# Three edits to a planned decoder kernel: mask order, cross-attention maxima from block-diagonal keys, a free choice of evicting engine

## The chip, the cores and the metric

One core of a Trainium2 chip. The time is device microseconds of one execution, the median of the runs shown. Before the change: 1095.75 us, from three runs of 1095.5, 1095.75 and 1112.12 us.

## What is computed

A decoder layer on x of 2 x 1024 tokens, 256 features, all in float32, in three residual steps:

```python
x = x + attn(layernorm(x))              # causal self-attention, then a "liquid" recurrence, then a GELU MLP
x = x + xattn(layernorm(x), ctx, ctx)   # cross-attention over 77 context tokens
x = x + ffn(layernorm(x))               # 8 binary trees of depth 7, each node a hidden unit
```

- `attn` works on two sequences of 1024 tokens with 16 heads of 16 features. Its scores are causal; the output is projected, the liquid step iterates `tanh(ctx @ w_ctx + xs @ w_x + b)` eight times, and an MLP of 1024 hidden units follows.
- `xattn` has 16 heads of 16 features as well, with 77 keys and values for each of the two sequences and no mask: `softmax(q k / 4) v`, then a projection.
- `ffn` has eight trees of 255 nodes; only the nodes on each token's path count.

A softmax here subtracts the row's maximum before the exponential. The largest edit concerns how cross-attention finds these maxima.

## The kernel before, in words

**Blocks and threads.** The 2048 tokens are cut into four blocks of 512 (`TB`). Each block has four chains of work, written as Python generators: `scores` (layernorm, query/key/value projections, the maxima of the causal scores), `values` (scores again with keys in the partitions, exponential, product with the values), `middle` (liquid recurrence, MLP, cross-attention, layernorm) and `leaves` (the trees). `prepare` runs once, ahead of block 0's `middle`, and makes a product of two weights (`w_ac`), a bias (`b_ac`), and the cross-attention's keys `xk` and values `xv`.

**The planner.** The order of instructions on PE (TensorE), ACT, DVE and POOL is fixed when the program is built. `Clock` keeps an account of when each engine, tile and PSUM bank would be free, by costs written into the class. `weave` (L283) looks at all chains, asks `choices` (L234) for what each could do next, and takes the step with the earliest start plus a "worth", ties going to the chain that is furthest behind its due place. DMAs all go through SP's queue in the order in which the program issues them.

**Heads in slots.** A head has 16 features, but each head's queries and keys stand in a slot of 32 partitions (`SLOT`), four heads to 128 partitions (`NG` = 4 groups). Odd rows hold features, row 0 holds the row maximum (in q) against a constant 1 (in k), so that the scores come out with the maximum subtracted. A product of one head is a matmul on 32 rows of PE's array. Four heads sit in four different row strips and run at the same time when they are issued one after the other. `Heads` (L68) describes such a unit; `choices` may issue two heads of one unit, four of one, or a mixed set: two heads of a unit that ACT will read (exponentials) and two of a unit that DVE will read (maxima). `issue` (L262) writes the matmuls. For a causal diagonal tile it first writes the mask into the bank as a bf16 matmul `mask x ident` over the whole array, step 0, and then accumulates the scores, step 1:

```python
for step in range(max(len(unit.steps) for unit, _, _ in heads)):
    for unit, j, ps in reversed(heads):
        if step < len(unit.steps):
            unit.one(j, ps, unit.steps[step])
```

**Cross-attention's maxima** (`cross_attention`, L897). Queries go through `project_slots` (L578): a projection into a tile, and four DMAs (L197) that spread it into the slots of `xq`. Then, for each of 4 pieces of 128 tokens (`qi`), one `Heads` unit makes 16 scores of 128 queries by 77 keys, one head at a time on 32 rows, four groups into the same bank of each head (L907). DVE reduces each bank, 4 x 77 columns to 4 maxima, four times; PE transposes the 512 maxima (L923), and `shift` (L652) puts them into row 0 of the queries: `q * head + pt`, where `head` is 0 in row 0 and 1 elsewhere. The exponentials' scores are made afterwards with the keys in the partitions (L948). There are 4 blocks x 4 pieces = 16 such rounds.

**Evictions.** A PSUM bank that only has to be copied out (with or without a scale and a bias) goes to a fixed engine: column half 0 to ACT, half 1 to DVE in `features_first` (L524) and `project_slots`; always to ACT in `weigh` (L609); one half each in `trees` (L999).

**Startup.** Weights are loaded in a fixed order (L394 to L412): `vecs`, block 0's x, `woT`, `w_ctx`, `wq`, `wk`, `wv`, `vrow` (five bias rows, 640 KB as broadcast), `ctxT`, `xwk`, `xwv` and the rest. `prepare` computes `w_ac`, then `b_ac`, then keys and values.

Of the kernel before, what the change touches and what calls it, by code (L numbers as in the profile page):

```python
# [40 lines left out]
for _name, _k in (  # L41
    ("g_attn", 2), ("b_attn", 2), ("bq", 2), ("bk", 2), ("out_b", 2), ("g1", 2), ("b1", 2),
    ("b_inl", 2), ("g2", 2), ("b2", 2), ("ff_b1", 8), ("xbq", 2), ("xbk", 4),
    ("b_in", 2 * PAR), ("rights", 2), ("shift", 1), ("head", 1),
):
    _COLS[_name] = (_n, _k)
    _n += _k
# [8 lines left out]
}  # L56

# [10 lines left out]
class Heads:  # L68
# [3 lines left out]
    def __init__(self, banks, one, read, engine, steps=(0,)):  # L72
        self.banks, self.one, self.read, self.engine, self.steps = banks, one, read, engine, steps
        self.left = [0, 2] if engine == "dve" else [2, 0]
        self.reads = []


class Clock:
# [10 lines left out]
    def __init__(self, nc):  # L89
        self.nc = nc  # L90
        self.pe = 0.0
        self.dma = 1.0
        self.at = {"act": 0.0, "dve": 0.0, "pool": 0.0, "dma": 0.0}
        self.written = {}
        self.used = {}
        self.banks = [0.0] * 8
        self.table = None
        self.mode = (P, P)
        self.share = 4
        self.children = []  # L100
# [49 lines left out]

    def transpose(self, out, x, ident):
        self.array(0.109, (P, P), out, x)
        return self.nc.tensor.transpose(out, x, ident)  # L153

    def array(self, cost, mode, out, *ins):
        cost += self.REARRANGE if (SLOT in mode or SLOT in self.mode) and mode != self.mode else 0.0
        self.mode = mode
        self.pe = max(self.pe, self.ready(ins) + self.HANDOVER) + cost
        self.note(self.pe + 0.14, out, ins)

# [38 lines left out]
    def load(self, out, src):  # L199
        self.dma = max(self.dma, self.pe - 6) + max(out.free_size() * 4 * P / 300e3, 0.5)  # L200
        self.note(self.dma + 2.0, out, ())
        self.nc.sync.dma_start(out=out, in_=src)
# [18 lines left out]
    def start(self, need):  # L221


        if isinstance(need, Op):
            return self.when(need)
        aps, kind = need
        if callable(kind):
            return self.pe if kind() else float("inf")
        at = max(self.pe, self.ready(aps) + self.HANDOVER)
        if kind:  # L230
            at = max(at, self.free_banks()[kind - 1][0])
        return at

    def choices(self, t, todo):  # L234

        need = t["need"]
        if isinstance(need, Op) or not isinstance(need[1], Heads):
            at = self.start(need)
            if isinstance(need, Op) or not need[0]:
                return [(at, 0.0, None)]  # L240
            return [(at, max(0.0, self.ready(need[0]) + self.MARGIN - at), None)]
# [7 lines left out]
        found.append((max(self.pe, ready, free[1][0]) + self.ALONE, 0.0, [(own, own.left[0])]))  # L249
        if len(own.left) == 2:  # L250
            found.append((two, 0.0, [(own, 0), (own, 2)]))
        for u in todo:
            other = None if isinstance(u["need"], Op) else u["need"][1]
            if not isinstance(other, Heads) or other.engine == own.engine:
                continue
            at = max(two, self.ready(u["need"][0]) + self.HANDOVER)
            for j0 in own.left:
                if 2 - j0 in other.left:
                    found.append((at, -self.MIXED, [(own, j0), (other, 2 - j0)]))
        return found  # L260

    def issue(self, heads):  # L262
# [5 lines left out]
        for step in range(max(len(unit.steps) for unit, _, _ in heads)):  # L268

            for unit, j, ps in reversed(heads):  # L270
                if step < len(unit.steps):
                    unit.one(j, ps, unit.steps[step])
# [10 lines left out]
    def weave(self, *threads):  # L283
# [25 lines left out]
        while todo:  # L309
# [9 lines left out]
            if heads:  # L319
                pe = self.pe = max(self.pe, at - self.ALONE if len(heads) == 1 else at)  # L320
                self.issue(heads)
                for t in todo:
                    if not isinstance(t["need"], Op):
                        share = sum(u is t["need"][1] for u, _ in heads) / len(heads)
                        t["done"][0] += share * (self.pe - pe)
            elif isinstance(need, Op):
                self.run(need)
# [14 lines left out]
def decoder_kernel(ctx: ExitStack, tc: tile.TileContext, ins: dict, out: bass.AP):  # L342
# [60 lines left out]
    vrow = const.tile([P, 5, D], F32, tag="vrow", name="vrow")  # L403
    clock.load(vrow.rearrange("p i d -> p (i d)"), ins["vrows"][0:1, :].to_broadcast([P, 5 * D]))
    ctxT = load("ctxT", (DC, B * T), **d)
    xwk = load("xwk", (DC, NG * P), **d)
    xwv = load("xwv", (DC, D), **d)
    wo = load("wo", (DC, D))
# [14 lines left out]
    mask32 = work.tile([P, P], F32, tag="mask32", name="mask32", bufs=1)  # L423
# [21 lines left out]
    xk = [const.tile([P, NG, T], F32, tag=f"xk{b}", name=f"xk{b}") for b in range(B)]  # L445
# [78 lines left out]
    def features_first(dst, src, name, g=None, b=None):  # L524

        for c in range(DC):
# [6 lines left out]
            if g is None:  # L533
                if c == 0:
                    yield clock.activation(dst[:, c, :], ps, AF.Copy)
                else:
                    yield clock.vector("tensor_copy", dst[:, c, :], ps)
            elif c == 0:
                yield clock.activation(dst[:, c, :], ps, AF.Identity, bias=col(b, c), scale=col(g, c))
            else:  # L540
                yield clock.vector("tensor_scalar", dst[:, c, :], ps, col(g, c), col(b, c), ALU.mult, ALU.add)
# [21 lines left out]
    def project_heads(dst, w, bias, src, n, name):  # L563

        for half in range(2):
            for i in range(2):
                g = 2 * half + i
                yield (src,), 2 if i == 0 else None
                if i == 0:
                    ps = banks(2)  # L570
                mm_cols(ps[i][:, :n], w, src, slice(g * P, (g + 1) * P), n)
                if i == 0:
                    yield clock.activation(dst(g), ps[i][:, :n], AF.Identity, bias=col(bias, g))
                else:
                    yield clock.vector("tensor_scalar", dst(g), ps[i][:, :n], col(bias, g), None, ALU.add)
            clock.free(*ps)

    def project_slots(dst, w, bias, src, tile, name):  # L578

        for c in range(DC):  # L580
# [3 lines left out]
            if c == 0:  # L584
                yield clock.activation(tile[:, c, :], ps, AF.Identity, bias=col(bias, c))
            else:
                yield clock.vector("tensor_scalar", tile[:, c, :], ps, col(bias, c), None, ALU.add)
# [7 lines left out]
    def project_values(dst, src, w, row, n, name):  # L595
# [3 lines left out]
        for c in range(DC):  # L599
# [4 lines left out]
            vrow[:n, row, :].rearrange("p (h d) -> p h d", d=HD),  # L604
# [4 lines left out]
    def weigh(at, av, g, name):  # L609
# [3 lines left out]
        yield clock.activation(raw, av, AF.Copy)  # L613
# [38 lines left out]
    def shift(q, pt):  # L652

        yield clock.vector("scalar_tensor_tensor", q, q, col("head", 0), pt, ALU.mult, ALU.add)


    def norms(tb, x, h0):
# [8 lines left out]
        yield from add_row(h0, 2)  # L666
        block[tb]["xn"] = xn

    def queries(tb):
# [9 lines left out]
        for i in range(NQ):  # L679
            cols = slice(i * P, (i + 1) * P)  # L680
            yield from project_values(v[:, blk * NQ + i], xn[:, :, cols], wv, 0, P, f"v{tb}_{i}")
# [58 lines left out]
    def weighted(tb, g, qT, at):  # L740
# [8 lines left out]
        def with_values():  # L749
            for kc in range(last + 1):  # L750
                yield (), lambda: step["made"] >= kc
                off = offset(kc)
                yield p[kc].values(), 1 if kc == 0 else None
# [109 lines left out]
    def feed_forward(tb, x, h0):  # L863
        hn = yield from layernorm(h0, f"l2_{tb}", "g2", "b2")
        yield clock.vector("tensor_tensor", x, x, h0, ALU.add)
        yield from add_row(x, 3)
# [30 lines left out]
    def cross_attention(tb, x):  # L897
        k, values = xk[tb // BPB], xv[tb // BPB]
        xn = yield from layernorm(x, f"x{tb}")
        yield from add_row(x, 4)  # L900
        yield from project_slots(xq, xwq, "xbq", xn, dtile(f"xqc{tb}"), f"xq{tb}")
        for qi in range(NQ):
            nm = nmax[2 + qi % 2]
            slots = nm.rearrange("p g (j s) -> p j g s", s=SLOT)
            cols = slice(qi * P, (qi + 1) * P)

            def scores(j, ps, g):  # L907
                r = slice(j * SLOT, (j + 1) * SLOT)
                clock.matmul(
                    ps[:, g * T : (g + 1) * T], xq[r, g, cols], k[r, g, :], start=True, stop=True  # L910
                )

            def read(j, ps):
                return [clock.vector(
                    "tensor_reduce", slots[:, j, :, 0],
                    ps[:, : NG * T].rearrange("p (g t) -> p g t", t=T), AX.X, ALU.max, negate=True,
                )]

            yield (xq[:, :, cols],), Heads(banks, scores, read, "dve", range(NG))
# [10 lines left out]
        def with_values():  # L930
            for g in range(NG):
                yield (), lambda: step["made"] >= g
                yield p[g].values(), 1
# [11 lines left out]
        for g in range(NG):  # L945
            p[g] = {}

            def one(j, ps, _):  # L948
                r = slice(j * SLOT, (j + 1) * SLOT)
                clock.matmul(ps[:T, :], k[r, g, :], xq[r, g, :], start=True, stop=True)  # L950
# [16 lines left out]
    def trees(tb):  # L967
# [5 lines left out]
        def outwards():  # L973


            for t in range(0, PAR, 2):
# [22 lines left out]
                if t == 0:  # L999
                    yield clock.activation(y[:, 0, :], po[0][:, :], AF.Copy)  # L1000
                    yield clock.vector("tensor_copy", y[:, 1, :], po[1][:, :])
# [48 lines left out]
    def prepare():  # L1050
        yield (woT, w_ctx), 2
        ps = banks(2)
        for dc in range(DC):
            for c in range(DC):
                clock.matmul(
                    ps[0][:, dc * D : (dc + 1) * D], woT[:, c, dc * P : (dc + 1) * P],
                    w_ctx[:, c, :], start=c == 0, stop=c == DC - 1,
                )
        yield clock.activation(w_ac, ps[0][:, :].rearrange("p (c d) -> p c d", d=D), AF.Copy)
        for oc in range(DC):  # L1060
            for c in range(DC):
                clock.matmul(
                    ps[1][:, oc : oc + 1], w_ctx[:, c, oc * P : (oc + 1) * P], col("out_b", c),
# [3 lines left out]
                b_ac[:, oc : oc + 1], ps[1][:, oc : oc + 1], col("b_inl", oc), None, ALU.add  # L1067
            )
        clock.free(*ps)
        for b in range(B):  # L1070
            src = ctxT[:, :, b * T : (b + 1) * T]
            yield from project_heads(lambda g: xk[b][:, g, :], xwk, "xbk", src, T, f"xk{b}")
            yield from project_values(xv[b][:, 0], src, xwv, 1, T, f"xv{b}")
# [107 lines left out]
def _arrays(a):  # L1181
# [13 lines left out]
        "rights": rights, "shift": shift, "head": 1 - shift,  # L1195
# [7 lines left out]
        "vrows": np.concatenate([bv, c["bv"], s["out_b"], s["ff_b2"], c["bo"]])[None],  # L1203
# [29 lines left out]
```

## Time and profile before

| what | value |
|---|---|
| median of the runs | 1095.75 us |
| the profiled execution's own time | 1099.84 us |
| its span, first to last instruction | 1098.1 us |
| mean granted TensorE clock | 0.972 |
| PE busy | 1022.7 us, 93% |
| weight loads (PEld) busy | 488.6 us, 44% |
| DVE busy | 648.6 us, 59% |
| ACT busy | 403.0 us, 37% |
| POOL busy | 81.2 us, 7% |
| HBM traffic over the span | 32 GB/s |

A float32 matmul stands in the trace as two MATMUL instructions (two passes), a bf16 matmul or a transpose as one. A row of a group reads: line, engine, operation, out<-in, shape, count, then busy time and mean duration, then the engine's idle time just before these instructions and what ended it. `32*128` is the part of the array in use, rows by columns. Line 149 is the helper that issues every matmul, line 153 every transpose, line 165 every activation, line 175 every DVE operation, so that groups are told apart by their tiles. "PEclk" is the clock that TensorE was granted, as a share of full speed.

### The profile page before, as it was taken

What the parts mean: (1) busy time and instruction counts of PE and PEld (TensorE: products, weight loads), DVE (VectorE), ACT (ScalarE), POOL (GpSimd) and SP (SyncE); (2) the same over time, 40 slices, a digit from 0 to 9 for tenths busy, and PEclk for the clock granted to TensorE, in tenths of its full rate; (3) what the DMA queues carried; (4) which work ended last, traced back from release to release, by engine and by line L of the source; (5) the groups of instructions that cost most, each with busy time, mean ns of one, the idle gap of its engine ahead of it and who ended that gap; (6) DMA issues with size and microseconds to landing.
All of it is one profiled execution on the core that took longest, in us unless ns stands there. A gap on an engine that the chain in (4) does not pass through costs nothing.

```text
span 1098.1 us, 14190 instructions
## 1 busy us (share of the span) xinstructions
PE 1022.7 (93%) x5496; PEld 488.6 (44%) x5496; DVE 648.6 (59%) x1369; ACT 403.0 (37%) x736; POOL 81.2 (7%) x161
## 2 busy tenths in 40 slices
PE   7899898998899999999998999998999999997798
PEld 5445333634336344554543334564334544643443
DVE  4665987156646787337576788445544687143444
ACT  4243234252481443334324354323455333214222
POOL 1122001010111101012000101000001000000000
PEclk9999998998999999999999999998999999986899
DMA  7202000200011000111110000121002001220020
GB/s 249 75 1 59 1 1 1 66 11 20 1 30 29 10 20 30 58 58 40 48 48 21 10 10 10 58 76 40 10 20 66 22 23 54 76 60 28 19 67 29
DMA packets 21618, 42.77 MB, mean 39 GB/s; under 512 B 2864, under 2 KB 3120, under 8 KB 21552
## 3 DMA queue, kind: packets, MB, share of 16 engines
q1 hardware_dynamic: 21552, 41.88, 12.6%
q8 instruction: 43, 0.70, 0.3%
q14 instruction: 23, 0.19, 0.1%
HBM read 33.48 MB, written 2.10 MB: 32 GB/s over the span
## 4 chain that ended last, share of the span: by engine, by line
PE 71%; DVE 8%; issue 8%; ACT 4%; DMA 1%; POOL 0%; POOLq 0%; SPq 0%; ACTq 0%; DVEq 0%
PE bank L149 67%; PE bank L153 4%; DVE top L175 3%; ACT p L165 2%; DVE ta L175 1%; DMA xq<-xqc 1%; DVE xn_l L175 1%; ACT ta L165 1%; DVE nmax L175 1%; DVE r L175 1%; ACT xp L165 1%; DVE w L175 1%; ACT th L165 0%; DVE x L175 0%; DVE h L175 0%
## 5 line engine op out<-in xcount | busy, mean ns | idle before, releaser
L165 ACT ACTIVATE p<-bank 128x512 f32<-128x512 f32 (+3 forms) x384 | 162.0, 494 | 197.2 <-PE bank L149 173.3
L175 DVE TENSOR_REDUCE top<-bank 128x1 f32<-128x512 f32 (+3 forms) x256 | 140.8, 583 | 75.7 <-PE bank L149 75.1
L149 PE MATMUL bank<-kT,qT 32*128 32x512 f32 (+3 forms) x768 | 133.7, 549 | 6.8 <-ACT p L165 4.3
L149 PE MATMUL bank<-qT,kT 32*128 32x512 f32 (+3 forms) x768 | 131.2, 539 | 5.9 <-ACT p L165 4.1
L149 PE MATMUL bank<-xn_t,trees 128*128 128x512 f32 x256 | 124.0, 611 | 0.5 <-DVE top L175 0.5
L175 DVE TENSOR_REDUCE nmax<-bank 128x4 f32<-128x308 f32 (+4 forms) x192 | 83.4, 479 | 68.5 <-PE bank L149 67.9
L149 PE MATMUL bank<-ta,trees 128*128 128x512 f32 x256 | 122.0, 606 | 0.1
L149 PE MATMUL bank<-w,w_dx 128*128 128x512 f32 x224 | 105.7, 605 | 5.4 <-DVE w L175 5.4
L165 ACT ACTIVATE th<-bank,half_b 128x512 f32<-128x512 f32 x64 | 44.0, 688 | 163.1 <-PE bank L149 163.1
L184 POOL TENSOR_SCALAR_AFFINE_SELECT p<-p 128x256 f32<-128x256 f32 x128 | 55.9, 442 | 516.6 <-ACT p L165 427.0
L149 PE MATMUL bank<-p,v 128*32 128x512 f32 (+3 forms) x768 | 86.4, 501 | 2.7 <-POOL p L184 2.5
L149 PEld LDWEIGHTS bank<-ta,trees 128*128 128x128 f32 x256 | 48.5, 194 | 55.0 <-issue 51.4
L165 ACT ACTIVATE w<-bank,b_ac 128x512 f32<-128x512 f32 x64 | 43.9, 689 | 75.9 <-PE bank L149 75.7
L149 PEld LDWEIGHTS bank<-xn_t,trees 128*128 128x128 f32 x256 | 47.5, 194 | 53.7 <-issue 45.6
L149 PEld LDWEIGHTS bank<-w,w_dx 128*128 128x128 f32 x224 | 39.9, 189 | 61.8 <-issue 45.2
L149 PEld LDWEIGHTS bank<-qT,kT 32*128 32x128 f32 x768 | 44.5, 186 | 44.0 <-ACT p L165 14.5
L149 PEld LDWEIGHTS bank<-kT,qT 32*128 32x128 f32 x768 | 44.3, 186 | 40.7 <-ACT p L165 12.0
L175 DVE TENSOR_TENSOR x<-x,bank 128x512 f32<-128x512 f32 x40 | 27.1, 683 | 58.9 <-PE bank L149 58.7
L149 PE MATMUL bank<-ff,ht 128*128 128x256 f32 x256 | 61.2, 382 | 0.0
L149 PE MATMUL bank<-xn_l,ff 128*128 128x512 f32 x128 | 60.8, 600 | 0.3 <-ACT xn_l L165 0.2
L175 DVE SCALAR_TENSOR_TENSOR ta<-ta,th 128x1024 f32<-128x1024 f32 x32 | 39.3, 1228 | 32.3 <-ACT ta L165 32.3
L149 PEld LDWEIGHTS bank<-ff,ht 128*128 128x128 f32 x256 | 48.0, 190 | 21.7 <-issue 16.8
(167 smaller groups left out, 1188.2 us busy)
## 6 DMA issues: line engine op xcount, KB each, us to landing
trees<-in_trees_dram SPq DMA_DIRECT2D x64, 256.0 KB, 2.7
ff<-in_ff_dram SPq DMA_DIRECT2D x32, 256.0 KB, 3.0
xn<-in_xtok_dram SPq DMA_DIRECT2D x4, 512.0 KB, 4.0
x<-in_xtok_dram SPq DMA_DIRECT2D x4, 512.0 KB, 4.6
qT<-qc SPq DMA_DIRECT2D x16, 128.0 KB, 2.3
kT<-kc SPq DMA_DIRECT2D x16, 128.0 KB, 2.4
xq<-xqc SPq DMA_DIRECT2D x16, 128.0 KB, 2.3
out_dram<-x SPq DMA_DIRECT2D x4, 512.0 KB, 3.1
```

What stands on the lines that cost most here:

```text
L149: return self.nc.tensor.matmul(out, w, x, **kw)
L153: return self.nc.tensor.transpose(out, x, ident)
L165: lambda: self.nc.scalar.activation(out, x, func, bias=bias, scale=scale),
L175: "dve", cost, 0.085, out, args, lambda: getattr(self.nc.vector, name)(out, *args, **kw)
L184: self.nc.gpsimd.affine_select(out=out, in_=args[0], **kw)
```

## The change

- **Mask order.** `issue` counts its steps downward, so that a unit with a mask writes it in the first round and the scores of all four heads come in the last one.
- **Cross-attention maxima.** The keys are stored block-diagonally: `xk[b]` becomes `[128, 4 groups, 4 heads, 77]`, and each head's block is zero outside its own 32 rows (`own`, four columns of ones and zeros). One matmul over all 128 rows then gives the scores of four heads, 128 queries by 308 columns, in one bank. A round is 4 such matmuls with a DVE reduction each, a plain step of the chain (one bank at a time) and no longer a `Heads` unit. `project_keys` replaces `project_heads`: one DVE operation per group adds the bias, copies four times and masks. The second scores read the head's own block, on the same 32 rows as before.
- **Evictions.** `evict` offers both an ACT and a DVE operation; `choices` takes the one that the account says is done first.
- **Account.** The switch between array shapes (`turn`) is now also a price in `choices`; loads are booked at 330 instead of 300 KB/us and from 1.8 us.
- **Others.** `shift` adds only. `b_ac` moves to the end of `prepare`. `vrow` loads four rows, and the fifth (`xrow`) is loaded by itself after `xwv`. The mask's float32 tile shares a pool.

```diff
         self.share = len(heads)
-        for step in range(max(len(unit.steps) for unit, _, _ in heads)):
+        for step in range(max(len(unit.steps) for unit, _, _ in heads), 0, -1):
 
             for unit, j, ps in reversed(heads):
-                if step < len(unit.steps):
-                    unit.one(j, ps, unit.steps[step])
+                if step <= len(unit.steps):
+                    unit.one(j, ps, unit.steps[-step])
...
+    def evict(self, out, ps, scale=None, bias=None):
+
+        if scale is None and bias is None:
+            return [
+                self.activation(out, ps, AF.Copy), self.vector("tensor_copy", out, ps)
+            ]
+        args = (bias, None, ALU.add) if scale is None else (scale, bias, ALU.mult, ALU.add)
+        return [
+            self.activation(out, ps, AF.Identity, bias=bias, scale=1.0 if scale is None else scale),
+            self.vector("tensor_scalar", out, ps, *args),
+        ]
...
+    def turn(self, mode):
+
+        return self.REARRANGE if SLOT in mode + self.mode and mode != self.mode else 0.0
...
         need = t["need"]
+        if isinstance(need, list):
+            need = t["op"] = min(need, key=lambda op: self.when(op) + op.cost + op.delay)
...
-            return [(at, max(0.0, self.ready(need[0]) + self.MARGIN - at), None)]
+            worth = max(0.0, self.ready(need[0]) + self.MARGIN - at) + self.turn((need[2:] or [FULL])[0])
+            return [(at, worth, None)]
...
-                    found.append((at, -self.MIXED, [(own, j0), (other, 2 - j0)]))
+                    worth = self.turn(max(own.mode, other.mode)) - self.MIXED
+                    found.append((at, worth, [(own, j0), (other, 2 - j0)]))
...
+    def project_keys(dst, w, bias, src, n):
+
+        for g in range(NG):
+            yield (src,), 1
+            ps = bank()
+            mm_cols(ps[:, :n], w, src, slice(g * P, (g + 1) * P), n)
+            at = _COLS["own"][0]
+            one, four = (ps[:, :n].rearrange("p (o t) -> p o t", o=1), [P, 4, n])
+            own = vecs[:, at : at + 4].rearrange("p (j o) -> p j o", o=1)
+            yield clock.vector(
+                "scalar_tensor_tensor", dst[:, g, :, :], one.to_broadcast(four), col(bias, g),
+                own.to_broadcast(four), ALU.add, ALU.mult,
+            )
+            clock.free(ps)
...
-        yield clock.vector("scalar_tensor_tensor", q, q, col("head", 0), pt, ALU.mult, ALU.add)
+
+        yield clock.vector("tensor_tensor", q, q, pt, ALU.add)
...
-            def scores(j, ps, g):
-                r = slice(j * SLOT, (j + 1) * SLOT)
+            for g in range(NG):
+                yield (xq[:, g, cols],), 1
+                ps = bank()
                 clock.matmul(
-                    ps[:, g * T : (g + 1) * T], xq[r, g, cols], k[r, g, :], start=True, stop=True
+                    ps[:, : 4 * T], xq[:, g, cols], k[:, g].rearrange("p j t -> p (j t)"),
+                    start=True, stop=True,
                 )
-
-            def read(j, ps):
-                return [clock.vector(
-                    "tensor_reduce", slots[:, j, :, 0],
-                    ps[:, : NG * T].rearrange("p (g t) -> p g t", t=T), AX.X, ALU.max, negate=True,
-                )]
-
-            yield (xq[:, :, cols],), Heads(banks, scores, read, "dve", range(NG))
+                yield clock.vector(
+                    "tensor_reduce", slots[:, g, :], ps[:, : 4 * T].rearrange("p (j t) -> p j t", t=T),
+                    AX.X, ALU.max, negate=True,
+                )
+                clock.free(ps)
```

## The prediction

> **What bounds the kernel now.** The page first: its busy line, PE's and the clock's slices, and the chain of work that ended last.
>
> ```profile
> PE 1022.7 (93%) x5496; PEld 488.6 (44%) x5496; DVE 648.6 (59%) x1369; ACT 403.0 (37%) x736; POOL 81.2 (7%) x161
> ...
> PE   7899898998899999999998999998999999997798
> ...
> PEclk9999998998999999999999999998999999986899
> ...
> PE 71%; DVE 8%; issue 8%; ACT 4%; DMA 1%; POOL 0%; POOLq 0%; SPq 0%; ACTq 0%; DVEq 0%
> ```
>
> PE bounds the kernel: busy 93%, 71% of the chain. So time can go in three ways: less work on PE, less idle time on it (1098.1 - 1022.7 = 75.4 us), or work done at a higher clock. The clock dips in a few slices, so I laid windows over the dips' neighbourhood. Columns: the window, PE busy, PEld, DVE, ACT, POOL, granted clock, DMA.
>
> ```profile
> 244.00:254.00 10.00, 10.00 (x73) 4.82 (x74) 6.94 (x13) 2.81 (x8) 1.96 (x4) 1.00 0.12 28
> 258.10:264.90 6.80, 5.39 (x23) 2.56 (x24) 4.37 (x9) 0.43 (x1) 0.00 (x0) 0.50 0.00 0
> ...
> 749.60:759.90 10.30, 8.44 (x47) 4.54 (x45) 7.45 (x15) 0.00 (x0) 0.00 (x0) 0.50 0.00 0
> ...
> 974.90:981.70 6.80, 6.26 (x23) 3.32 (x24) 2.95 (x6) 0.00 (x0) 0.00 (x0) 0.50 0.09 20
> ...
> 992.00:1009.00 17.00, 13.21 (x80) 5.64 (x84) 4.26 (x9) 6.83 (x12) 0.00 (x0) 0.50 0.00 0
> ```
>
> Four stretches, 41 us together, run at exactly half the clock. Each begins during or just after the cross-attention maxima of a block (`bank<-xk,xq`). PE's timeline shows why, in the last block, where nothing else is left to fill in:
>
> ```profile
> 986.82 1.13 PE L149 MATMUL bank<-xk,xq 32*128 32x77 f32 x32
> 989.71 0.66 PE L153 MATMUL bank<-ident,nmax 128*128 128x128 f32 x4 [1.76 <-DVE nmax L175]
> 990.29 1.13 PE L149 MATMUL bank<-xk,xq 32*128 32x77 f32 x32
> 993.18 1.11 PE L153 MATMUL bank<-ident,nmax 128*128 128x128 f32 x4 [1.76 <-DVE nmax L175]
> 994.23 2.00 PE L149 MATMUL bank<-xk,xq 32*128 32x77 f32 x32
> ```
>
> All 16 small products come at once (1.13 us, 2.00 at half clock), then PE waits 1.76 us for four reductions in a row. The waits confirm it: the largest is on `nmax`, and `xq`'s DMA is another of this stage.
>
> ```profile
> PE bank L153 <- DVE nmax L175: 14.0, 8, 2.1
> PE bank L149 <- ACT p L165: 12.0, 18, 1.3
> ...
> PE bank L149 <- DMA xq<-xqc: 6.5, 6, 2.3
> ```
>
> Over the five stretches that hold these maxima (253.8 to 266.7, 506 to 524, 745 to 756.5, 776 to 788, 972.4 to 999.9) the windows' sum is 81.90 us with PE busy 64.02: 17.9 us idle.
>
> [...]only 0.50 and 1.00 here, in stretches of 3.4, 6.8, 10.2 and 17.1 us. [...] Here the second pass of a four-head set of 512 columns, followed by another mode, takes about 0.52 us to the next start, and 0.43 within full-array work: about 0.09 us a change.
>
> **The change, part by part.**
>
> *Product work of the maxima.* Before: 16 rounds x 1.13 us = 18.1 at full clock. After: 16 x 4 float32 products of 308 columns on 128 rows, two passes each. The trace has no such shape; starts of `xn_l,ff` (512 columns) are 0.429 us apart, of `ff,ht` (256) 0.216, so 308 takes 0.258. 64 x 2 x 0.258 = 33.0 us. That is +14.9, on PE, the bound. Below, 0.25 from 256 columns upward (+13); above, all at half clock (+48).
>
> *Mode changes.* In the built order of instructions, PE changes between full, row-strip and column-strip work 485 times before and 461 times after. 24 x 0.09 = -2.2 us. Here is the effect of the maxima's new mode and of `turn`.
>
> *Sets of heads.* The other scores pair differently, since the maxima no longer take places in sets and `choices` pays for turns. I grouped them in the built order by strips that can run together: 221 sets before, 219 after, with the widest members summing to 95,744 and 92,032 columns. Two passes of 0.429 / 512 = 0.84 ns a column: -6.2 us.
>
> *Masks first.* Nothing. In the built order before, every mixed set with masks already reads mask, mask, exponential scores, maxima scores; after, mask, mask, maxima scores, exponential scores. The unit with the mask was written first in its round anyway, as ACT's unit is the one that owns the pair. Four heads run together in both. The bound is zero both ways, within the 7 ns between neighbouring starts.
>
> *Waits around the maxima.* After, each product has its own bank, and DVE reduces it (four in a row take 1.64 in the trace) while PE does the next (0.52). In three blocks the built order has other products between almost all of them, so only the last block keeps waits: three of some 0.75 us (the last reduction of 0.47, and handovers), 2.3 us. `xq`'s DMAs are the same four per block, landing 2.3 us after issue, and the first product needs only the first half; I keep 4 of 6.5. 17.9 - 6.3 = -11.6 us. Ends: -5 if the last block gains nothing, -17 if all goes.
>
> *Clock.* In the four half-clock stretches PE was busy 5.39 + 8.44 + 6.26 + 13.21 = 33.3 us, which full clock would do in half: -16.7 at most. A round is now 4 x 0.516 = 2.06 us of full-array products and the transposes' 0.66 in about 3.3 us, well above the 1.13 + 0.66 in 3.5 that went before the last stretch. Against it: from 1000 us on ACT's exponentials (6.83 us busy) pace the stretch. I take -12; bounds 0 and -16.7.
>
> *Evictions.* By the built order 31 evictions leave DVE for ACT and 7 go the other way: 24 x about 0.75 us (`xqc` 0.75, `xaT` 0.69) = 18 us off DVE, on to ACT at 0.60 to 0.69 each. ACT is busy 37%, so its share lies under PE's work; if ACT were late instead, the queue behind it is the exponentials (12.0 us of PE's waits already). PE waits for DVE outside the maxima for some 20 us (`w` 5.4, `xc_t` 5.0, `top` 5.0 and less); I take -3. Bounds +5 and -8.
>
> *Startup.* Before, `b_ac` stood in DVE's queue ahead of block 0's layernorm and idled DVE 3.62 us to 12.17. After, the layernorm runs on and PE waits for `xwk`, whose load has 128 KB less ahead of it. Scores begin at 32.8 us; PE is busy 17.95 of 20 us from 20 to 40, so most of it is work: -1.5. The eight key operations on DVE (nearest row: `ta<-bank,vecs_sb,ta` 0.741 for 512 columns, so about 0.47 for 308) replace four of 0.29 and four on ACT: +2.6 us of DVE under PE's projections. `xrow` is one more load of 128 KB, on SP behind `xwv`; `vrow` is that much shorter. If DVE's cover were gone: +2.6.
>
> *`shift`.* 32 additions, 0.68 (`x<-x,bank`) instead of 0.745: below 2 us on DVE, counted above.
>
> Sum: +14.9 - 2.2 - 6.2 - 11.6 - 12 - 3 - 1.5 = -21.6 us. The profiled span 1098.1 becomes 1076.5, its own time 1078.2. The profiled execution lies 4.1 us above the median of the runs; taken off the median, 1095.75 - 21.6 = 1074.1.
>
> **Rivals.**
>
> *The clock dips stay, or come elsewhere.* [...]other dips (at 186.4, 579.0, 1015.9 and 1026.1 us, 20.4 us together) show that attention's and layernorm's waits cause them too. Then -21.6 + 12 = -9.6: 1086. For it: fewer fillers remain in the last block. Against it: three of the four big dips sit on the removed pattern.
>
> *More comes off than counted.* With DVE relieved those other dips vanish too (PE busy 17.26 us in them, half of it 8.6) and some of the other waits (75.4 - 17.9 - 7.7 at the start = 50 us): -32, 1064. For it: dips follow waits. Against it: the 4.8 us wait for the last block's layernorm (`xc_t`) isn't touched.
>
> *Slower: full-array products at half clock.* The maxima's products stay in half-clock stretches and the waits stay, as new work simply moves them. Half clock doubles 33.0. Without the gains of waits, clock and evictions the sum is +14.9 - 2.2 - 6.2 - 1.5 = +5.0; slower by 2% (21.9 us) needs 17 us more, that is half of the products at half clock. At 60%: +25, 1121.
>
> *An edit that does nothing:* the mask order, as worked out. It is part of every case.
>
> **How the numbers follow.** Likeliest, 0.55: 1074, own range 1065 to 1083. Dips stay: 0.2 (1086). More: 0.2 (1064). Slower: 0.05. The line of 2%, about what a measurement of this kernel can tell from no change, is 1073.8, in the middle of the likeliest case: half of it and all of the 0.2 below give 0.48 for faster; 0.47 same; 0.05 slower. Range for 8 in 10: 1059 to 1089.
>
> **What would show it.** Right: PEclk without the dips at 258, 750 and 975 to 1009; the wait on `nmax` below 5 us; `bank<-xk,xq` x128 of 308 columns with some 33 us of starts; DVE busy about 18 us less, ACT's more; PE busy share up to 95%. Wrong: the products at a mean far above 0.43 us each (half clock), a new large wait of PE on ACT, or the dips at new places.

## The result, and the profile after

The changed kernel takes 1086.25 us (median of 4 runs, 1084.51 to 1089.82) against 1099.32 us for the kernel before, run on the same chip: a ratio of 0.9855, 95% interval 0.9809 to 0.9901. That is 1.0 to 1.9% faster, less than 2%. The ratio is formed from fast runs alone and is not the quotient of the two medians, which is 0.988. The forecast was 1074.0 with a range of 1059 to 1089, so the time lies inside the range, near its upper end, where the rival "the dips stay" had stood (1086). Its mechanism isn't that rival's, though: most of the dips did go. The profiled execution took 1086.23 us of its own, span 1084.5.

The page of the changed kernel, in the lines that answer to those of before:

```profile
PE 1014.0 (94%) x5098; PEld 486.6 (45%) x5112; DVE 633.0 (58%) x1349; ACT 420.8 (39%) x756; POOL 79.4 (7%) x161
...
PE   6899888998999999999989999999997999998798
...
PEclk9999999999999999999999999999999999999899
...
PE 50%; issue 6%; DVE 3%; ACT 1%; DMA 0%; POOL 0%; POOLq 0%; DVEq 0%; ACTq 0%
```

PE's busy time fell by 8.7 us although the change adds work to PE: of the five eights and the six in the clock row, one eight is left. PE's idle time, span less busy, fell from 75.4 to 70.5 us only. DVE lost 15.6 us and ACT gained 17.8, as the count of evictions said.

PE's waits in the changed kernel (us in total, times, longest):

```profile
PE bank L153 <- DVE top L195: 12.5, 27, 1.1
PE bank L169 <- DVE xc_t L195: 10.1, 3, 4.8
...
PE bank L153 <- ACT p L185: 4.8, 8, 1.1
PE bank L169 <- DVE nmax L195: 3.6, 4, 2.1
...
PE bank L153 <- DMA xq<-xqc: 1.9, 1, 1.9
```

The wait on `nmax` was 14.0 at this place and is 3.6; `xq`'s DMA was 6.5 and is 1.9; `p` was 12.0 and is 4.8. But `top`, the reductions of the causal maxima, rose from 5.0 to 12.5, and `xc_t`, the layernorm ahead of the trees, from 5.0 to 10.1. The two lines of before:

```profile
PE bank L153 <- DVE xc_t L175: 5.0, 2, 4.8
PE bank L149 <- DVE top L175: 5.0, 12, 0.9
```

The rise of `xc_t` is one event. PE's timeline near it, and a window over the clock at that place:

```profile
840.50 2.29 PE L169 MATMUL bank<-ident,xc_t 128*128 128x128 f32 x8 [4.78 <-DVE xc_t L195]
```

```profile
838.50:845.30 6.80, 4.80 (x15) 3.82 (x16) 1.86 (x7) 1.19 (x2) 0.90 (x1) 0.50 0.00 0
```

PE stands 4.78 us for a chain of statistics on DVE and POOL, with nothing else planned there, and the clock halves. Before, such a wait stood only at the end, where it still is (1014.4):

```profile
1028.15 2.30 PE L153 MATMUL bank<-ident,xc_t 128*128 128x128 f32 x8 [4.77 <-DVE xc_t L175]
```

The maxima themselves, by groups with shapes apart, and the last block in PE's timeline:

```profile
L153 PE MATMUL bank<-xk,xq 128*128 128x308 f32 x128 | 42.8, 437 | 1.9 <-DMA xq<-xqc 1.9
```

```profile
982.85 2.24 PE L153 MATMUL bank<-xk,xq 128*128 128x308 f32 x8
984.93 0.55 PE L169 MATMUL bank<-ident,nmax 128*128 128x128 f32 x3
985.66 0.33 PE L169 MATMUL bank<-ident,nmax 128*128 128x128 f32 x1 [0.19 <-DVE nmax L195]
985.83 2.24 PE L153 MATMUL bank<-xk,xq 128*128 128x308 f32 x8
```

The 437 ns of one include the modelled end; the starts lie mostly 0.259 us apart, where the prediction had estimated 0.258. A round in the last block is now 2.98 us (982.85 to 985.83) with 0.19 us of waiting, instead of 3.47 with 1.76.

### The profile page after: what moved, and what is told of

The parts are those of the page before. It is cut to its first block, busy times and chain, and to the rows that moved or that the text cites. A ratio compares the mean times of both kernels' runs of the same rounds, so it can differ in the third digit from the quotient of the medians.

```text
span 1084.5 us, 13443 instructions
## 1 busy us (share of the span) xinstructions
PE 1014.0 (94%) x5098; PEld 486.6 (45%) x5112; DVE 633.0 (58%) x1349; ACT 420.8 (39%) x756; POOL 79.4 (7%) x161
## 3 DMA queue, kind: packets, MB, share of 16 engines
q1 hardware_dynamic: 21696, 41.88, 12.5%
## 4 chain that ended last, share of the span: by engine, by line
PE 50%; issue 6%; DVE 3%; ACT 1%; DMA 0%; POOL 0%; POOLq 0%; DVEq 0%; ACTq 0%
PE bank L153 47%; PE bank L169 3%; DVE top L195 1%; DVE ta L195 1%; ACT ta L185 0%; ACT xp L185 0%; DMA trees<-in_trees_dram 0%; ACT p L185 0%; ACT th L185 0%; DVE x L195 0%; DVE stats_x L195 0%; DVE stats_t L195 0%; ACT raw_x L185 0%; POOLq L1252 0%; POOL rs_t L206 0%
## 5 line engine op out<-in xcount | busy, mean ns | idle before, releaser
L153 PE MATMUL bank<-qT,kT 32*128 32x512 f32 (+3 forms) x768 | 134.5, 537 | 4.4 <-ACT p L185 2.3
L195 DVE TENSOR_REDUCE nmax<-bank 128x4 f32<-128x308 f32 (+4 forms) x192 | 85.8, 480 | 88.9 <-PE bank L153 87.6
L153 PE MATMUL bank<-xn_t,trees 128*128 128x512 f32 x256 | 121.4, 601 | 0.2
L153 PE MATMUL bank<-ta,trees 128*128 128x512 f32 x256 | 119.3, 594 | 0.4
L153 PE MATMUL bank<-w,w_dx 128*128 128x512 f32 x224 | 102.7, 598 | 5.3 <-DVE w L195 5.3
L153 PE MATMUL bank<-p,v 128*32 128x512 f32 (+3 forms) x768 | 84.1, 500 | 4.0 <-POOL p L204 3.4
```

Source lines behind the costliest of these rows:

```text
L153: return self.nc.tensor.matmul(out, w, x, **kw)
L195: "dve", cost, 0.085, out, args, lambda: getattr(self.nc.vector, name)(out, *args, **kw)
```

## The experiments

Five numbers of each kernel's profile are set beside its time below: PE's work, its idle time (span less busy), and its waits on `p`, on `xc_t` and on `top`. "Work" is PE's busy time less half of what falls into half-clock stretches, an estimate of the busy time at full clock: in the trace of before, products of `ta,trees` start 0.429 us apart at full clock and 0.853 at half. "Clock" is the mean granted clock over all runs of the kernel, not of the profiled one alone. Ratios are against the kernel before on the same chip, whose medians were 1099.32 to 1102.91. A profile shows one run: that of e4 was the slowest of its six (1085.62 us), that of e12 the fastest of its six (1106.16).

| kernel | median us | ratio [95%] | clock (runs) | PE work | PE idle | `p` | `xc_t` | `top` |
|---|---|---|---|---|---|---|---|---|
| before | 1102.91 | 1 | 0.967 (59) | 997.4 | 75.4 | 12.0 | 5.0 | 5.0 |
| before, reordered (e9) | 1099.03 | 0.997 [0.9947, 0.9992] | 0.974 (22) | 994.2 | 76.9 | 11.6 | 4.8 | 5.6 |
| before, filler (e6) | 1097.91 | 0.9948 [0.9925, 0.9972] | 0.979 (22) | 1003.1 | 69.4 | 10.2 | 9.7 | 6.4 |
| keys alone (e1) | 1108.04 | 1.0046 [1.0028, 1.0064] | 0.984 (22) | 1016.0 | 77.1 | 8.0 | 12.6 | 6.9 |
| keys alone, reordered (e12) | 1112.2 | 1.0103 [1.0069, 1.0137] | 0.983 (6) | 1015.3 | 77.8 | 9.4 | 10.2 | 6.1 |
| all but keys (e2) | 1090.64 | 0.9875 [0.9834, 0.9916] | 0.979 (6) | 985.2 | 82.4 | 6.8 | 9.5 | 11.0 |
| all but keys and turn price (e7) | 1100.35 | 0.9977 [0.9958, 0.9995] | 0.980 (22) | 1002.4 | 76.4 | 6.6 | 5.0 | 5.1 |
| all but evictions (e3) | 1096.51 | 0.9942 [0.991, 0.9973] | 0.990 (10) | 1015.2 | 70.4 | 9.2 | 5.0 | 4.4 |
| all but masks first (e5) | 1096.36 | 0.9955 [0.9935, 0.9975] | 0.986 (22) | 1009.7 | 74.0 | 9.8 | 9.1 | 6.1 |
| all but masks first and turn price (e10) | 1103.73 | 1.0022 [1.0001, 1.0043] | 0.985 (22) | 1012.0 | 77.0 | 8.1 | 11.6 | 7.6 |
| after | 1086.25 | 0.9855 [0.9809, 0.9901] | 0.989 (4) | 1004.2 | 70.5 | 4.8 | 10.1 | 12.5 |
| after, reordered (e8) | 1081.4 | 0.9814 [0.9778, 0.9849] | 0.990 (5) | 1003.5 | 64.4 | 4.7 | 4.8 | 11.3 |
| all but turn price (e4) | 1080.33 | 0.9791 [0.9753, 0.9829] | 0.991 (6) | 1007.8 | 62.1 | 5.2 | 4.8 | 4.0 |
| all but turn price, reordered (e11) | 1083.16 | 0.9834 [0.9801, 0.9867] | 0.992 (5) | 1008.6 | 65.1 | 6.6 | 4.8 | 5.8 |

**The keys alone.** The changed kernel with its other three edits taken back (the startup's are kept):

```diff
...
-        for step in range(max(len(unit.steps) for unit, _, _ in heads), 0, -1):
+        for step in range(max(len(unit.steps) for unit, _, _ in heads)):
...
-                yield clock.evict(dst[:, c, :], ps)
+                yield clock.evict(dst[:, c, :], ps)[c]
...
-        found.append((one, self.turn(own.mode), [(own, own.left[0])]))
+        found.append((one, 0.0, [(own, own.left[0])]))
...
```

> The changed kernel with the mask order, the free evictions and the price of a mode change in the planner's choices undone: of the change, the block-diagonal keys and the new startup stay. Theory A (the keys bring the gain: half-clock stretches and waits around the maxima go, at the price of some 15 us of product work): ratio to before 0.982 to 0.992, half-clock time under 30 us, PE's wait on nmax and xq's DMA together under 8 us. Theory B (the keys cost what they save, and the gain comes from the planner's new freedom): ratio 0.997 or above.

1108.04 us: the theory that the keys by themselves bring the gain fell. Their local effect is there. PE's waits in this kernel:

```profile
PE bank L169 <- DVE xc_t L195: 12.6, 3, 4.8
PE bank L153 <- ACT p L185: 8.0, 14, 1.1
PE bank L153 <- DVE w L195: 7.7, 10, 1.7
...
PE bank L153 <- DVE top L195: 6.9, 16, 0.7
...
PE bank L169 <- DVE nmax L195: 3.3, 5, 2.1
```

`nmax` fell as in the changed kernel, and `p` by 4.0, but `xc_t` rose by 7.6, `w` by 2.3 and `top` by 1.9. PE idles 77.1 us, not 75.4: the waits changed places. The clock rose (0.967 to 0.984), but PE's work rose by 18.6 us (997.4 to 1016.0), and that is more than the clock gives back.

**The keys undone.** The changed kernel with the old maxima, 16 products of 32 rows and 77 columns a round as a `Heads` unit, read from the block-diagonal keys.

```diff
...
                 clock.matmul(
-                    ps[:, : 4 * T], xq[:, g, cols], k[:, g].rearrange("p j t -> p (j t)"),
-                    start=True, stop=True,
+                    ps[:, g * T : (g + 1) * T], xq[r, g, cols], k[r, g, j, :], start=True, stop=True
                 )
...
```

> The changed kernel with the maxima made head by head on row strips again (the keys stay stored block-diagonally, each head reads its own block); mask order, evictions and account stay. Theory A: ratio to before 0.995 to 1.01, half-clock time above 45 us, waits on nmax of 10 us or more. Theory B: ratio 0.980 to 0.990.

0.9875: nearly all of the gain is still there, as the second theory had it, although the half-clock time (48 us) and the wait on `nmax` (9.8 us) are back. PE:

```profile
PE 1005.8 (92%) x5482; PEld 484.7 (45%) x5496; DVE 634.3 (58%) x1355; ACT 416.6 (38%) x750; POOL 81.1 (7%) x161
```

It idles 82.4 us. Busy time hides what the keys do, since it holds the half-clock stretches too. By the table's work, 985.2 us here and 1004.2 with the keys, they add 19 us of products, and take off 12 us of waiting and 11 us of half clock. Little is left of it.

**The evictions fixed.** Every `evict(...)` is followed by `[c]`, `[0]` or `[oc]` (the first diff shows one of these places), so that the eviction goes to its fixed engine of before; nothing else.

> The changed kernel with evictions on the fixed engines of before. The changed kernel's PE waits 13 us on top and 10 us on xc_t where before it waited 5 and 5. If the free choice of engine brought these waits: idle time of PE falls by 6 to 10 us, ratio to before 0.976 to 0.981. If the order of the other work did: ratio within 0.004 of 0.9855, waits on top above 10 us still.

0.9942 against 0.9855: the free choice is worth 0.9% here, about 10 us instead of the 3 predicted. Both expectations missed: the waits on `top` and `xc_t` do fall, to 4.4 and 5.0 us, but the kernel is slower.

```profile
PE 1025.4 (94%) x5103; PEld 486.6 (44%) x5112; DVE 648.0 (59%) x1373; ACT 402.8 (37%) x732; POOL 80.1 (7%) x161
```

```profile
PE bank L153 <- ACT p L185: 9.2, 15, 1.1
...
PE bank L153 <- DMA ff<-in_ff_dram: 5.1, 3, 2.8
```

Nor do the longer waits on `p` explain it: PE idles 70.4 us here and 70.5 in the changed kernel. What differs is PE's busy time, 1025.4 against 1014.0, and half clock isn't the reason (PE is busy for 20.3 and 19.6 us of these stretches).

**The price of a turn left out.**

```diff
...
-            worth = max(0.0, self.ready(need[0]) + self.MARGIN - at) + self.turn((need[2:] or [FULL])[0])
+            worth = max(0.0, self.ready(need[0]) + self.MARGIN - at)
...
-                    worth = self.turn(max(own.mode, other.mode)) - self.MIXED
+                    worth = -self.MIXED
...
```

> The changed kernel without the price of a mode change in the planner's choices (the account of matmuls keeps it). The built order has 496 changes of mode instead of 461 and sets of heads that are as full (92,800 columns, 92,032). By product work alone: 35 x 0.09 = +3.2 us, + 1.3 for the columns: ratio to before 0.988 to 0.991. If the price had brought the new waits on top (it prefers sets of one mode, one after the other, and DVE falls behind): ratio 0.978 to 0.983, waits on top near 5 us.

1080.33 us, 0.9791, the lowest time of all. Two of its waits:

```profile
PE bank L169 <- DVE xc_t L195: 4.8, 1, 4.8
PE bank L153 <- DVE top L195: 4.0, 11, 0.8
```

`top` is back at 4.0 us, and the layernorm wait at 840 us is gone, because a product of the trees is planned into it.

**Masks upward.** The first hunk of the first diff alone.

> The changed kernel with the steps of a set counted upward again: mask, mask, exponential scores, maxima scores. If the mask order does nothing, as predicted: ratio to before within 0.004 of the changed kernel's 0.9855 (the built order is otherwise nearly the same; 991.1 us of work on PE by the order, 990.2). If the order matters because DVE's scores, written ahead of ACT's, let DVE's bank be awaited earlier: waits of PE on top fall from 12.5 to 5 us, ratio 0.977 to 0.981.

0.9955 against 0.9855: the order of the masks, which I had put at nothing, is worth 1.0% here. Neither expectation came: `top` fell from 12.5 to 6.1 us, and the kernel got slower. PE's work is 5.5 us longer and its idle time 3.5.

**A filler in the kernel before.** Three useless products of 256 columns (`xwq` by itself, into the bank that the transposes use next) in each of the four rounds of the last block, between the maxima's products and the transposes that wait for `nmax`. It computes more than the reference needs, and changes no output.

```diff
...
-            yield (nm,), 1
+            yield (xq[:, :, cols],), 1
             pt = bank()
+            for i in range(3 if tb == NTB - 1 else 0):
+                clock.matmul(pt[:, :D], xwq[:, 0, :P], xwq[:, 1, :], start=True, stop=True)
+            yield (nm,), None
...
```

> The kernel before with three useless products of 256 columns (1.3 us of PE) between the scores and the transposes of each of the four rounds of maxima in the last block; nothing else differs, and the outputs don't depend on them. If the half-clock stretches beside the maxima come from PE's waiting for the reductions and cost what I said: the stretches between 975 and 1009 (24 us) go, and the time falls by 3 to 9 us although 5.2 us of work are added (ratio 0.992 to 0.997). If half clock costs nothing there (ACT and DVE pace this stage) or isn't set by PE's activity: ratio 1.000 to 1.005.

PE's timeline, and the window that ran at half clock before:

```profile
993.99 1.13 PE L149 MATMUL bank<-xk,xq 32*128 32x77 f32 x32
995.05 1.56 PE L149 MATMUL bank<-xwq_sb 128*128 128x256 f32 x6
996.88 0.66 PE L153 MATMUL bank<-ident,nmax 128*128 128x128 f32 x4 [0.27 <-DVE nmax L175]
997.46 1.13 PE L149 MATMUL bank<-xk,xq 32*128 32x77 f32 x32
```

```profile
992.00:1009.00 17.00, 15.28 (x139) 8.14 (x137) 7.53 (x16) 7.27 (x14) 0.00 (x0) 1.00 0.13 47
```

With 5.2 us of useless work (24 passes of 0.216) the kernel is 0.3 to 0.8% faster, as the first theory had it. The small products take 1.13 us in the rounds shown, and the wait of 1.76 is 0.27 (the filler stands in it). The test isn't pure: the planner also set products of the trees among the first rounds, and other dips came, so that half-clock time in the profile is 58 us, hardly less than before. Over the 22 runs the mean clock is 0.979 instead of 0.967. So the local effect is shown; the 0.5% is no more than an order alone moves, as the next but one experiment finds.

**All but keys and turn price.** The diffs of the second and fourth experiments together, to see evictions and masks without the keys.

> The changed kernel with the maxima on row strips again and without the price of a mode change: of the change, the free evictions, the mask order and the new startup stay. After the first four runs the free evictions look like the gain (fixed: 0.9942 instead of 0.9855; keys undone: 0.9875). If the keys add nothing on top of them: ratio to before 0.975 to 0.984, as with the keys (0.9791). If the keys do add, once turns are free: ratio 0.988 or above.

0.9977: almost nothing. With the keys the same two edits give 0.9791, so here the keys are worth 1.9%, and by themselves less than nothing. PE's work differs by only 5.4 us in these two profiles, where the keys cost 19 in the two pairs above. The parts don't add up.

**An order changed by one constant.** How much of all this is accident? `EACH`, the width of a block in the planner's due times, was set from 220 to 218: the same work in a slightly other order.

```diff
-    EACH = 220
+    EACH = 218
```

> The changed kernel with the due times of the four chains scaled by 218 / 220 in the planner: the same work (989.4 us on PE by the built order, 990.2), in another order. If the planner's orders of equal quality give equal times: ratio to before within 0.003 of 0.9855. If the order's small accidents are worth as much as the edits (the changed kernel's new waits on xc_t and top being such accidents): ratio off by 0.005 or more, either way, with other waits at the top of the list.

> The kernel before with one constant of the order changed (EACH = 218 for 220): the same work in a slightly other order, so it measures how far an order alone moves the time of the kernel before. Theory A (the gain of the whole change is more than such an accident): within 0.6% of before, ratio 0.994 to 1.006, waits of TensorE 64 to 78 us. Rival (the gain is an accident of order, as large as what any reorder brings): outside of that, 0.985 to 0.994 or 1.006 to 1.015.

> The changed kernel without the price of a mode turn, with EACH = 218. Theory A (the price of a turn in the choice costs, by holding back the transposes and products that others wait for): again faster than the changed kernel of the same constant (1081.4 us, ratio 0.981), 1074 to 1080 us, ratio 0.974 to 0.980. Rival (its 0.6% was an accident of order): 1081 to 1090 us, 0.981 to 0.989.

> The block-diagonal maxima alone (masks upward, evictions fixed, no price of a turn), with EACH = 218; with 220 it took 1108.04 us, ratio 1.0046. Theory A (without free evictions the waits that the maxima lose come back at the layernorms and at the normalised output, so the keys alone bring nothing): 1098 to 1110 us, ratio 0.996 to 1.007. Rival (that was an accident of order; the keys by themselves take off what was predicted of them): 1080 to 1093 us, ratio 0.980 to 0.991.

The four pairs differ by 0.3% (before), 0.4% (after), 0.4% (without the turn price) and 0.6% (keys alone). The profile of the reordered after shows what such an accident is: it lost the layernorm wait at 840 us, 4.8 us. Another is a wait on the load of `ff`, 4.6 to 5.8 us in all: e3, e4, e5, e7, e10, e11 and e12 have it, the others not, and e1 and e12 differ by the constant alone. Of the expectations, the one on the changed kernel came out between its two cases (0.0041 off), the one on the kernel before came out as the first theory had it, the one on the turn price as the rival had it, and the keys alone were slower than either said. So a difference up to some 0.6% can't be put down to an edit. The turn price, 0.6% worse at 220 and 0.2% better at 218, isn't told from nothing. That the keys alone bring no gain, and that the whole change does, stands in both orders: 1.0046 and 1.0103 against 0.9855 and 0.9814.

**Masks again, without the turn price.**

> The changed kernel with its masks counted upward again and the price of a mode turn left out of the choice; to be read against the changed kernel without the price alone (1080.33 us, ratio 0.979) and against the one with the masks undone alone (1096.36 us, 0.9955). Theory A (masks first is worth about 1% of itself, whatever the order around it): 1090 to 1096 us, ratio 0.988 to 0.994. Rival (the 1% of the masks was an accident of order): 1077 to 1085 us, ratio 0.976 to 0.984.

1.0022, against 0.9791 with masks first: 2.3%, after 1.0% the first time. Both are above what an order alone has moved. Neither theory had it so large.

```profile
PE bank L169 <- DVE xc_t L195: 11.6, 3, 4.8
PE bank L153 <- ACT p L185: 8.1, 16, 0.9
...
PE bank L153 <- DVE top L195: 7.6, 18, 0.9
```

These three are 6.8, 2.9 and 3.6 us longer than with masks first, 13.3 of the 14.9 us by which PE idles longer. 4.8 of the 6.8 are a layernorm wait in mid-run again, an accident of order by the experiment before, and no kernel with masks upward was run in a second order. So 1.0 and 2.3% are two measured differences, and how much of them belongs to the edit is open.

## Why the prediction was near, and where it failed

The sum of the profiled executions: own time 1099.84 to 1086.23, -13.6 instead of -21.6.

| term | predicted | found |
|---|---|---|
| products, turns, sets of heads | +6.5 | +6.8 |
| waits on `nmax` and `xq`'s DMA | -11.6 | -15.2 |
| clock | -12 | -15.5 |
| all other idle time of PE (evictions, startup) | -4.5 | +10.3 |
| masks first | 0 | no line of its own, part of those above |

**The level.** The -21.6 was taken off 1095.75, the median of three runs. The 59 runs of the kernel before have 1102.91, and 0.9855 of that is 16.0 us less. So of the 12 us between 1074.1 and 1086.25 about 7 lie in a base that was low by chance, and about 5 in the sum.

**Work on PE: right in sum, its split not shown.** The price of the new shape was right (0.258 us a pass, 0.259 measured). The 0.09 us of a mode change comes out of the changed kernel's trace too, as about 0.1: the second pass of a four-head set of 512 columns takes 0.54 us to the next start where full-array or column-strip work follows (31 cases), and 0.43 where another set follows (5 cases). But the keys alone raise PE's work by 18.6 us (21.1 in the other order), and the other three edits take 11.8 off again. The prediction gave -8.4 to turns and sets. With keys, turn price and masks first, but fixed evictions, the work is still 17.8 us above before, although PE changes mode 466 times there, close to the 461 of the changed kernel. So in this pair the free evictions go with 11 us less work, which no term had, and that the sum comes out at +6.8 is partly luck. Where these 11 us lie isn't shown; waits too short for the trace to tell from work may be among them.

**Clock: right, and 3.5 us more than predicted.** Half-clock stretches fell from 61.3 to 23.8 us in the two profiles. PE was busy for 50.7 and 19.6 us of them; by the spacing of starts above, full clock would have saved about half of that, an estimated 25.3 and 9.8. The repeated runs say it without a model: in 59 runs of the kernel before, clock and time go together (correlation -0.93), 0.80 us for each 0.001 of mean clock, and the mean is 0.967 before and 0.989 after. The filler agrees, though its gain is no more than an order alone moves: the some 12 points of 0.001 that it gained make 9.6 us at that slope; less the 5.2 us of its work that is -4.4, and -5.0 was measured. The first rival, that the dips stay or come elsewhere, is out as a whole. But of the 23.8 us, 13.6 lie where the profile of before has none (39.8, 162.7 and 838.5 us), which the prediction had named as a sign of being wrong. That the new rounds would run at full clock was my estimate; in the last block they did, with PE busy for 14.73 of 16.00 us at a clock of 1.00 (975 to 991 us). Before, PE was busy for 7.97 of 10.30 us (981.7 to 992.0) ahead of the half-clock stretch. At what busy share the clock falls isn't shown.

**Waits around the maxima: right at their place, wrong as a term of the sum.** The step said that 17.9 - 6.3 us of idle time come off the total. They come off that place. In the keys alone they came back in full elsewhere: PE's idle time is 77.1 and 77.8 us in both orders, 75.4 and 76.9 before. With masks first and free evictions beside them, the keys take off 11.9 us (82.4 to 70.5) and 14.3 us (76.4 to 62.1), about as predicted. I treated a wait as if the rest of the order stayed in place. But the products that used to stand near it can move with it, and then lack at the next place with nothing to do, such as the layernorm at 840 us.

**"Evictions: I take -3" and what was left out beside it: the step that failed.** The idle time outside the maxima rose by 10.3 us: 7.5 on `top`, 5.1 on `xc_t`, a gain of 7.2 on `p`, and 4.9 in small waits, 1.8 of them on the load of `xwk`. I had the other waits fall with DVE's load. They don't: PE idles as long with fixed evictions as with free ones (70.4 and 70.5 us), and what the free ones bring in this pair is in PE's busy time. The startup gave less than its 1.5: PE's first scores of the causal part start at 32.7 us instead of 33.1. The `xc_t` part is the layernorm wait, an accident of order: the reordered version and the two without the turn price don't have it. `top` goes with the turn price where masks come first and evictions are free: 12.5, 11.0 and 11.3 us with the price, 4.0, 5.1 and 5.8 without. Yet the time at 218 was no worse with the price, so part of that wait is only moved.

**"Masks first. Nothing": not what was measured.** On PE it is nothing: a mixed set with masks and a pair of 512 columns takes mostly 1.26 to 1.28 us from the first mask to the next start in both kernels, whichever pair is written first. But the order also enters the account, which books the pair written second 0.53 us later (two of 0.263 us for 512 columns) than the first. The edit changes when the planner believes the maxima's and the exponentials' scores to be there, and so the order of all that follows. One wait separates the kernels accordingly: the five with the new keys that lack masks first, free evictions or both wait 8.0 to 9.8 us for `p`, the six that have both, with or without the keys, 4.7 to 6.8. These few microseconds are less than the 10 to 23 us between the kernels. That the account's picture of readiness is the cause is argued, not shown; an experiment that changes the booking alone, and not the order on PE, was not made.

**Which of the four parts brought the gain** has no answer as a sum. Taken back one at a time they are worth 0.2% (keys; 1.9% without the turn price), 0.9% (evictions), 1.0% (masks; 2.3% without the turn price) and -0.6 to +0.2% (turn price). The evictions' 0.9% is a single pair, hardly above what an order moves. The versions at 0.979 to 0.983 are not told apart by their intervals.

## What to carry to other kernels

Where a planner fixes the order, an edit's local wait is only gained if the work that it sets free finds a place where PE would stand idle; ask for the next place with nothing to do. Measure PE's total idle time rather than the wait that you removed, and beside it the busy time without the half-clock part: with evictions fixed the kernel was 0.9% slower at the same idle time. Before a part is credited with half a per cent, change a constant of the order that should do nothing, and see how far the time moves (here 0.3 to 0.6%). An edit that costs nothing on the engine can still go with a change of 1% or more, through the order that the planner makes of it.

## What the runs showed of the hardware

- Rounds of 3.47 us with 1.76 us of waiting each led into 17 us at half clock, from 992 us on; with 1.3 us of useless products in each round, and products of the trees in the first ones, the same window ran at full clock. In the traces of before and after PE waits three times for 4.3 us or more on `xc_t` (before: from 1023.4 us; after: from 835.7 and 1009.6), and each time a stretch of 6.8 us at half clock follows, beginning 2.7 to 2.9 us after the wait does.
- The half-clock stretches of the trace of before are 3.4, 6.8, 10.2 and 17.1 us long, those of the changed kernel 3.4 and 6.8. In each of the two traces they begin whole multiples of 3.413 us apart.
- Runs of one kernel often differ with the mean granted clock: by 0.80 us for each 0.001 in the kernel before (59 runs, correlation -0.93), by 1.03 in the one with masks upward (22 runs, -0.93); in the keys alone the two go together less (22 runs, -0.47).
- Four heads in four row strips start together: in the trace of before, groups of four passes start within 18 to 39 ns of each other, with a median of 20.
- In a mixed set of two and two heads in four row strips, each pair goes on at its own width. In the traces of before and after the four first passes mostly start within 20 ns (95 of 100 sets), the second passes of a pair of 128, 256 or 384 columns mostly at about 0.42, 0.53 or 0.64 us after the first mask, those of a pair of 512 at 0.74 to 0.75. With such a pair the set mostly takes 1.26 to 1.28 us with its masks, whatever the other pair's width.
